# One fused attention and FFN layer: another order of head and loads, and a last FFN in token halves

## The chip, the cores and the metric

The kernel runs on one core of one Trainium2 chip. It is written for a scheduler that places instructions on five engines: TensorE (PE, matrix products), VectorE (DVE), ScalarE (ACT), GpSimd (POOL) and SyncE (SP, which here only issues transfers). The metric is the time on the device in microseconds (us), as a median of several runs. The profile is of one execution; its span is a little shorter than the time.

## The reference

What is computed, cut to what matters (`x` is 4 x 2048 tokens of 256 numbers, FFN weights are integers from -127 to 127):

```python
# attention within chunks of C = 32 tokens
Q = x @ W_q.T;  K = x @ W_k.T;  V = x @ W_v.T
decay = sigmoid(log_decay[0])
mask = where(diff >= 0, decay ** diff, 0)        # diff = position - position, 32 x 32
S = einsum('bncd,bnkd->bnck', Qc, Kc) * mask
O = einsum('bnck,bnkd->bncd', S, Vc)
gate = sigmoid(x @ W_g.T)
x = layernorm(x + ((gate * O) @ W_o.T + x))
# FFN with hidden size 768, weights scaled by 1/127
gate, up = x @ wg.T, x @ wu.T
x = layernorm(x + (silu(gate) * up) @ wd.T)
```

## The kernel before

The 8192 tokens are worked on in 16 blocks of 512. `Q K^T` is computed as `x (W_q^T W_k) x^T`, so a product `m` of the two weights is made once (`pm`), and a block needs `py` (x times m), `pg` (gate), `pv` (values), `ps` (scores), `po` (scores times values), `pa` (output product), then the first norm and `pt` (transposes). The FFN uses a faster single-pass format for its products. To keep precision, each activation is split in a high and a low part (`hT_hi`, `hT_lo`; `u_hi`, `u_lo`), and each product is done for both. The weights are exact integers there, as long as none is above 4096; the kernel counts the partitions with a larger one (`n_wide`) and would recompute everything in a second way if there were any.

Pools and banks (`bufs` is how many tiles of one name exist at once):

```python
xin = tc.tile_pool(name="xin", bufs=3)
work = tc.tile_pool(name="work", bufs=2)          # yT, sg, v, sT, goT, r, h, s, u, o ...
acts = tc.tile_pool(name="acts", bufs=H // P + 2) # u_hi, u_lo: 8 each
psum = tc.tile_pool(name="psum", bufs=8, space=PSUM)   # all products share 8 banks of 128 x 512
```

Loads at the start, in this order:

```python
wq = load_w(nc.sync, w_q, "wq")
wk = load_w(nc.scalar, w_k, "wk")
xs = {0: load_x(0)}                # xT, then x, both on nc.sync
wg = load_w(nc.scalar, w_gT, "wg")
wv = load_w(nc.scalar, w_vT, "wv")
nc.gpsimd.dma_start(decay, log_decay[0:1, 0:1].to_broadcast([P, 1]))
wo = load_w(nc.scalar, w_oT, "wo")
xs[1] = load_x(1)
ffn_int = [load_w(nc.sync, w, name) for ...]     # three of 768 KB
```

Then `pm` and its copy `m_sb`, the mask (some forty small DVE operations), and the loop:

```python
def integers(w_int, name):
    t = const.tile(list(w_int.shape), F32R, ...)
    nc.vector.tensor_copy(t, w_int)
    return t

def look_for_wide():
    for i, w_int in enumerate(ffn_int):
        nc.vector.tensor_reduce(top[:, i : i + 1], w_int..., ALU.max, apply_absolute_value=True)
    nc.vector.tensor_scalar(wide, top, EXACT, None, ALU.is_gt)
    nc.tensor.matmul(pw[:1, :3], lhsT=ones, rhs=wide, start=True, stop=True)
    nc.vector.tensor_reduce(count, pw[:1, :3], ..., ALU.add)
    nc.vector.tensor_copy(n_wide, count)

for b in range(-1, NB):            # attention of block n = b + 1 between parts of the FFN of b
    n = b + 1
    ffn, attn = b >= 0, n < NB
    ...
    if attn:
        yT, sg, v = attn_project(n)          # py, pg, pv
        sT = attn_scores(n, yT)              # ps
    if b == -1:
        fg, fu, fd = (integers(w, name) for ...)
        n_wide = look_for_wide()
    if ffn:  ffn_up(b, hT, uT, half[0])      # chunks 0 to 2 of the hidden size
    if attn: goT = attn_values(n, sT, v, sg) # po
    if ffn:  ffn_up(b, hT, uT, half[1])      # chunks 3 to 5
    if attn: h_next = attn_out(n, goT)       # pa, first norm
    if ffn:  r = ffn_down(b, uT, h)          # fdn
    if attn: h, hT = h_next, transpose_h(n, h_next)   # pt
    if ffn:  finish(b, r)                    # second norm, store of 512 KB
```

One chunk of the FFN, and the norm:

```python
# ffn_up, per chunk of 128 hidden units: fg and fu, 4 products of 512 columns each, then
nc.scalar.activation(s, pg, AF.Sigmoid, scale=SCALE)
nc.vector.tensor_tensor(s, pg, s, ALU.mult)
nc.vector.tensor_tensor(u, pu, s, ALU.mult)
nc.scalar.copy(hi, u)
nc.gpsimd.tensor_tensor(lo, u, hi.bitcast(F32), ALU.subtract)

# layer_norm, for the 4 groups of 128 tokens of a block
nc.vector.bn_stats(st, r[:, g, :]); nc.vector.bn_aggr(mv[:, g, :], st)     # per group
nc.scalar.activation(rstd, mv[:, :, 1], AF.Sqrt, bias=eps)                 # once
nc.vector.reciprocal(rstd, rstd)                                           # once
nc.vector.tensor_scalar(dst[:, g, :], r[:, g, :], mv..., rstd..., ALU.subtract, ALU.mult)  # per group
```

Of the kernel before, what the change touches and what calls it, by code (L numbers as in the profile page):

```python
# [34 lines left out]
P = 128  # L35
# [3 lines left out]
SCALE = 1.0 / 127.0  # L39
EXACT = 4096.0  # L40
EPS = 1e-5


@with_exitstack
def kernel(
# [32 lines left out]
        return psum.tile([P, TB], F32, tag="ps", name=name)  # L78


    def load_x(b, start=None):
        tokens = slice(b * TB, (b + 1) * TB) if start is None else bass.ds(start, TB)
        xt = xin.tile([P, KD, TB], F32, tag="xT", name=f"xT_{b}")
        nc.sync.dma_start(xt, xT[:, tokens].rearrange("(k p) t -> p k t", p=P))
        xn = xin.tile([P, NG, D], F32, tag="x", name=f"x_{b}")
        nc.sync.dma_start(xn, x[tokens, :].rearrange("(g p) d -> p g d", p=P))
        return xt, xn

    def load_w(eng, w, name):
        k, n = w.shape[0] // P, w.shape[1]  # L90
# [1 line left out]
        eng.dma_start(t, w.rearrange("(k p) n -> p k n", p=P))  # L92
        return t

    wq = load_w(nc.sync, w_q, "wq")
    wk = load_w(nc.scalar, w_k, "wk")
    xs = {0: load_x(0)}
    wg = load_w(nc.scalar, w_gT, "wg")
    wv = load_w(nc.scalar, w_vT, "wv")
    decay = const.tile([P, 1], F32, tag="decay", name="decay")  # L100
    nc.gpsimd.dma_start(decay, log_decay[0:1, 0:1].to_broadcast([P, 1]))
    wo = load_w(nc.scalar, w_oT, "wo")
    if NB > 1:
        xs[1] = load_x(1)
    ffn_int = [
        load_w(nc.sync, w, name)
        for w, name in ((ffn_gT, "fg_int"), (ffn_uT, "fu_int"), (ffn_dT, "fd_int"))
    ]

    ident = const.tile([P, P], F32, tag="ident", name="ident")  # L110
    make_identity(nc, ident)
# [2 lines left out]


    m_sb = const.tile([P, KD, D], F32, tag="m", name="m_sb")
    pm = bank("pm")
    for ec in range(KD):
        for dc in range(KD):
            nc.tensor.matmul(  # L120
                pm[:, ec * D : (ec + 1) * D],
                lhsT=wq[:, dc, ec * P : (ec + 1) * P],
                rhs=wk[:, dc, :],
                start=(dc == 0),
                stop=(dc == KD - 1),
            )
    nc.vector.tensor_copy(m_sb.rearrange("p k n -> p (k n)"), pm)  # L127

# [34 lines left out]

    def integers(w_int, name):
        t = const.tile(list(w_int.shape), F32R, tag=name, name=name)
        nc.vector.tensor_copy(t, w_int)
        return t

    def look_for_wide():

        top = const.tile([P, len(ffn_int)], F32, tag="top", name="top")
        for i, w_int in enumerate(ffn_int):
            nc.vector.tensor_reduce(  # L175
                top[:, i : i + 1],
                w_int.rearrange("p k n -> p (k n)"),
                mybir.AxisListType.X,
                ALU.max,
                apply_absolute_value=True,  # L180
            )
        wide = const.tile([P, len(ffn_int)], F32, tag="wide", name="wide")
        nc.vector.tensor_scalar(wide, top, EXACT, None, ALU.is_gt)
        ones = const.tile([P, 1], F32, tag="ones", name="ones")
        nc.vector.memset(ones, 1.0)
        pw = bank("pw")
        nc.tensor.matmul(pw[:1, : len(ffn_int)], lhsT=ones, rhs=wide, start=True, stop=True)
        count = const.tile([1, 1], F32, tag="count", name="count")
        nc.vector.tensor_reduce(
            count, pw[:1, : len(ffn_int)], mybir.AxisListType.X, ALU.add  # L190
        )
        n_wide = const.tile([1, 1], I32, tag="n_wide", name="n_wide")
        nc.vector.tensor_copy(n_wide, count)
        return n_wide

    def layer_norm(dst, r, name):

        mv = small.tile([P, NG, 2], F32, tag="mv", name=f"mv_{name}")
        for g in range(NG):
            st = small.tile([P, 6], F32, tag="st", name=f"st_{name}_{g}")  # L200
            nc.vector.bn_stats(st, r[:, g, :])
            nc.vector.bn_aggr(mv[:, g, :], st)
        rstd = small.tile([P, NG], F32, tag="rstd", name=f"rstd_{name}")
        nc.scalar.activation(rstd, mv[:, :, 1], AF.Sqrt, bias=eps)
        nc.vector.reciprocal(rstd, rstd)
        for g in range(NG):
            nc.vector.tensor_scalar(
                dst[:, g, :],
                r[:, g, :],
                mv[:, g, 0:1],  # L210
                rstd[:, g : g + 1],
                ALU.subtract,
                ALU.mult,
            )


    def attn_project(b):
        xt, _ = xs[b]
        yT = work.tile([P, KD, TB], F32, tag="yT", name=f"yT_{b}")
        sg = work.tile([P, KD, TB], F32, tag="sg", name=f"sg_{b}")  # L220
        v = work.tile([P, NG, D], F32, tag="v", name=f"v_{b}")
        for fc in range(KD):
            py = bank(f"py_{b}_{fc}")
            for ec in range(KD):
# [5 lines left out]
                    stop=(ec == KD - 1),  # L230
                )
            nc.vector.tensor_copy(yT[:, fc, :], py)
        for dc in range(KD):
            pg = bank(f"pg_{b}_{dc}")
            for ec in range(KD):
                nc.tensor.matmul(  # L236
                    pg,
                    lhsT=wg[:, ec, dc * P : (dc + 1) * P],
                    rhs=xt[:, ec, :],
                    start=(ec == 0),  # L240
                    stop=(ec == KD - 1),
                )
            nc.scalar.activation(sg[:, dc, :], pg, AF.Sigmoid)
        per = TB // D
        for h in range(NG // per):
            pv = bank(f"pv_{b}_{h}")
# [10 lines left out]
            nc.scalar.copy(  # L257
                v[:, h * per : (h + 1) * per, :].rearrange("p g d -> p (g d)"), pv
            )
        return yT, sg, v  # L260

    def attn_scores(b, yT):
        xt, _ = xs[b]
        ps = bank(f"ps_{b}")
        for g in range(NG):
            cols = slice(g * P, (g + 1) * P)
# [50 lines left out]
        return t[:, gs, :].rearrange("p g d -> p (g d)")  # L317

    def attn_out(b, goT):
        _, xn = xs.pop(b)  # L320
        r = work.tile([P, NG, D], F32, tag="r1", name=f"r1_{b}")

        def residual(gs, pb):
# [23 lines left out]
        return hi, lo  # L347


    def ffn_up(b, hT, uT, chunks):  # L350
        for hc in chunks:
            pg = bank(f"fg_{b}_{hc}")
            pu = bank(f"fu_{b}_{hc}")
            for pb, w in ((pg, fg), (pu, fu)):
                terms = [(dc, part) for dc in range(KD) for part in hT]
                for i, (dc, part) in enumerate(terms):
                    nc.tensor.matmul(  # L357
                        pb,
                        lhsT=w[:, dc, hc * P : (hc + 1) * P],
                        rhs=part[:, dc, :],  # L360
                        start=(i == 0),
                        stop=(i == len(terms) - 1),
                    )
            s = work.tile([P, TB], F32, tag="s", name=f"s_{b}_{hc}")
            nc.scalar.activation(s, pg, AF.Sigmoid, scale=SCALE)  # L365
            nc.vector.tensor_tensor(s, pg, s, ALU.mult)  # L366
            u = work.tile([P, TB], F32, tag="u", name=f"u_{b}_{hc}")
            nc.vector.tensor_tensor(u, pu, s, ALU.mult)  # L368
            hi = acts.tile([P, TB], F32R, tag="u_hi", name=f"u_hi_{b}_{hc}")
            lo = acts.tile([P, TB], F32R, tag="u_lo", name=f"u_lo_{b}_{hc}")  # L370
            nc.scalar.copy(hi, u)  # L371
            nc.gpsimd.tensor_tensor(lo, u, hi.bitcast(F32), ALU.subtract)  # L372
            uT[0].append(hi)
# [12 lines left out]
        return r  # L386

    def finish(b, r, start=None):
        tokens = slice(b * TB, (b + 1) * TB) if start is None else bass.ds(start, TB)
        o = work.tile([P, NG, D], F32, tag="o", name=f"o_{b}")  # L390
        layer_norm(o, r, f"f{b}")
        nc.sync.dma_start(
            out[tokens, :].rearrange("(g p) d -> p g d", p=P), o
        )


    half = list(range(KH // 2)), list(range(KH // 2, KH))
    h = hT = None
    for b in range(-1, NB):
        n = b + 1  # L400
        ffn, attn = b >= 0, n < NB
        if n + 1 < NB and n + 1 not in xs:
            xs[n + 1] = load_x(n + 1)
        if ffn:
            uT = [], []
        if attn:
            yT, sg, v = attn_project(n)
            sT = attn_scores(n, yT)
        if b == -1:
            fg, fu, fd = (  # L410
                integers(w, name) for w, name in zip(ffn_int, ("fg", "fu", "fd"))
            )
            n_wide = look_for_wide()
        if ffn:
            ffn_up(b, hT, uT, half[0])
        if attn:
            goT = attn_values(n, sT, v, sg)
        if ffn:
            ffn_up(b, hT, uT, half[1])
        if attn:  # L420
            h_next = attn_out(n, goT)
        if ffn:
            r = ffn_down(b, uT, h)
        if attn:
            h, hT = h_next, transpose_h(n, h_next)
        if ffn:
            finish(b, r)


    def wide_block(start, weights):  # L430

        wide_g, wide_u, wide_d = weights
        xs["w"] = load_x("w", start)
        yT, sg, v = attn_project("w")
        goT = attn_values("w", attn_scores("w", yT), v, sg)
        h = attn_out("w", goT)
        hT = work.tile([P, KD, TB], F32, tag="hT_hi", name="hT_w")
        for dc in range(KD):
# [86 lines left out]
```

## Time and profile before

| what | before |
|---|---|
| time, median of 3 runs | 599.48 us (598.05 to 599.63) |
| span of the profiled execution | 596.3 us |
| busy share of PE, DVE, ACT, POOL | 96%, 62%, 37%, 21% |
| mean granted clock of PE | 0.988 |
| transfers in the span | 29.36 MB, 49 GB/s on average |

The profile gives, for each engine, when it was busy and what released it after each wait. "PEld" is the load of stationary weights into TensorE, beside the products. A product of 32-bit numbers appears as two or more matmul records, and matmuls overlap, so that the pace from start to start is what counts and not the length of one record. A wait line names the engine and the tile that waited, whom it waited for, and the total, the number and the longest of the waits. The chain that ended last is followed back from the last instruction; in the order of time, each of its rows has a start, a length and what was done.

### The profile page before, as it was taken

How to read it: one execution, taken by the hardware profiler on the slowest of the kernel's cores; microseconds unless marked ns; L12 is line 12 of the kernel's file. 1: busy time of each engine (PE TensorE's matmuls, PEld its weight loads, DVE VectorE, ACT ScalarE, POOL GpSimd, SP SyncE). 2: the span in 40 equal slices, each digit the busy share in tenths (PEclk: the TensorE clock that was granted, in tenths of full speed). 3: DMA queues.
4: the chain of work that ended last, by engine and by line, in shares of the span. 5: the costliest groups of instructions: out<-in, count | busy, mean ns of one | idle time of the engine just before them, and what ended most of it. 6: DMA issues, size and time to landing. Idle time of an engine off the chain costs nothing.

```text
span 596.3 us, 7549 instructions
## 1 busy us (share of the span) xinstructions
PE 572.0 (96%) x2954; PEld 459.5 (77%) x2954; DVE 368.0 (62%) x843; ACT 220.6 (37%) x357; POOL 125.3 (21%) x107
## 2 busy tenths in 40 slices
PE   5589999999999999999999999999999999999994
PEld 3457878788787878878787896878878787887883
DVE  3853756748475674747568474765847477583784
ACT  0213335333343433334343333533333352334472
POOL 1000404022040412205031130502213040220422
PEclk9889999999999999999999999999999999999998
DMA  8611111211201111120211211021121101001011
GB/s 276 217 36 35 36 36 36 72 35 36 71 24 48 36 49 59 35 71 2 71 36 35 71 37 51 21 71 36 37 70 36 35 1 37 1 1 35 1 36 38
DMA packets 24006, 29.36 MB, mean 49 GB/s; under 512 B 928, under 2 KB 19360, under 8 KB 23968
## 3 DMA queue, kind: packets, MB, share of 16 engines
q1 hardware_dynamic: 22848, 27.79, 14.5%
q10 hardware_dynamic: 1088, 1.05, 0.5%
q8 instruction: 25, 0.41, 0.3%
q14 instruction: 13, 0.11, 0.1%
q0 software_dynamic: 32, 0.00, 0.0%
HBM read 20.45 MB, written 8.39 MB: 48 GB/s over the span
## 4 chain that ended last, share of the span: by engine, by line
PE 91%; DVE 4%; DMA 3%; ACT 1%; issue 0%; POOL 0%; POOLq 0%; SPq 0%; DVEq 0%
PE fdn L304 15%; PE fg L357 14%; PE fu L357 14%; PE pa L304 9%; PE py L225 9%; PE pv L250 9%; PE pg L236 9%; PE po L285 5%; PE ps L268 4%; PE pt L340 2%; DMA fg_int<-in_ffn_gT_dram 2%; DVE top L175 1%; DMA wk<-in_w_k_dram 1%; DVE u L368 0%; DVE mask L163 0%; DVE s L366 0%
## 5 line engine op out<-in xcount | busy, mean ns | idle before, releaser
L372 POOL TENSOR_TENSOR u_lo<-u,u_hi 128x512 fp32r<-128x512 f32 x96 | 123.4, 1285 | 458.7 <-ACT u_hi L371 458.2
L365 ACT ACTIVATE s<-fg 128x512 f32<-128x512 f32 x96 | 57.5, 599 | 106.4 <-PE fg L357 106.4
L366 DVE TENSOR_TENSOR s<-fg,s 128x512 f32<-128x512 f32 x96 | 66.4, 692 | 48.6 <-ACT s L365 48.6
L304 PE MATMUL fdn<-fd,u_hi 128*128 128x256 f32 x384 | 95.3, 292 | 0.0
L304 PE MATMUL fdn<-fd,u_lo 128*128 128x256 f32 x384 | 92.7, 280 | 1.2 <-POOL u_lo L372 1.2
L357 PE MATMUL fg<-hT_hi,fg 128*128 128x512 f32 x192 | 78.7, 410 | 0.2 <-ACT hT_hi L343 0.2
L357 PE MATMUL fu<-hT_hi,fu 128*128 128x512 f32 x192 | 76.3, 397 | 0.0
L357 PE MATMUL fg<-hT_lo,fg 128*128 128x512 f32 x192 | 76.1, 396 | 0.0
L357 PE MATMUL fu<-hT_lo,fu 128*128 128x512 f32 x192 | 76.0, 396 | 0.0
L276 DVE TENSOR_TENSOR sT<-ps,mask 128x512 f32<-128x512 f32 x16 | 11.1, 691 | 105.2 <-PE ps L268 105.2
L368 DVE TENSOR_TENSOR u<-fu,s 128x512 f32<-128x512 f32 x96 | 66.4, 692 | 13.1 <-DVE s L366 0.5
L304 PEld LDWEIGHTS fdn<-fd,u_lo 128*128 128x128 f32 x384 | 72.4, 189 | 2.0 <-POOL u_lo L372 1.6
L304 PEld LDWEIGHTS fdn<-fd,u_hi 128*128 128x128 f32 x384 | 71.8, 188 | 0.4
L371 ACT CAST u_hi<-u 128x512 fp32r<-128x512 f32 x96 | 59.0, 614 | 34.7 <-DVE u L368 34.7
L225 PE MATMUL py<-xT,m_sb 128*128 128x512 f32 x128 | 58.5, 600 | 1.0 <-DVE m_sb L127 1.0
L250 PEld LDWEIGHTS pv<-wv,xT 128*128 128x128 f32 x256 | 48.7, 190 | 13.4 <-issue 7.6
L304 PE MATMUL pa<-wo,goT 128*128 128x256 f32 x256 | 58.2, 380 | 0.0
L250 PE MATMUL pv<-wv,xT 128*128 128x256 f32 x256 | 57.9, 379 | 0.0
L236 PE MATMUL pg<-xT,wg 128*128 128x512 f32 x128 | 57.5, 593 | 0.0
L304 PEld LDWEIGHTS pa<-wo,goT 128*128 128x128 f32 x256 | 48.7, 191 | 7.3 <-DVE goT L292 0.4
L236 PEld LDWEIGHTS pg<-xT,wg 128*128 128x128 f32 x128 | 24.4, 190 | 30.6 <-issue 30.6
L357 PEld LDWEIGHTS fu<-hT_hi,fu 128*128 128x128 f32 x192 | 36.1, 188 | 8.8
(68 smaller groups left out, 657.9 us busy)
## 6 DMA issues: line engine op xcount, KB each, us to landing
xT<-in_xT_dram SPq DMA_DIRECT2D x16, 512.0 KB, 3.7
x<-in_x_dram SPq DMA_DIRECT2D x16, 512.0 KB, 3.6
out_dram<-o SPq DMA_DIRECT2D x16, 512.0 KB, 2.9
fg_int<-in_ffn_gT_dram SPq DMA_DIRECT2D x1, 768.0 KB, 10.9
fu_int<-in_ffn_uT_dram SPq DMA_DIRECT2D x1, 768.0 KB, 9.6
fd_int<-in_ffn_dT_dram SPq DMA_DIRECT2D x1, 768.0 KB, 11.4
wk<-in_w_k_dram ACTq DMA_DIRECT2D x1, 256.0 KB, 4.2
wq<-in_w_q_dram SPq DMA_DIRECT2D x1, 256.0 KB, 3.9
```

The costliest lines, as they stand in the source:

```text
L225: nc.tensor.matmul(py, lhsT=m_sb[:, ec, fc * P : (fc + 1) * P], rhs=xt[:, ec, :], start=(ec == 0), stop=(ec == KD - 1),)
L236: nc.tensor.matmul(pg, lhsT=wg[:, ec, dc * P : (dc + 1) * P], rhs=xt[:, ec, :], start=(ec == 0), stop=(ec == KD - 1),)
L250: nc.tensor.matmul(pv[:, j * D : (j + 1) * D], lhsT=xt[:, ec, g * P : (g + 1) * P], rhs=wv[:, ec, :], start=(ec == 0), stop=(ec == KD - 1),)
L268: nc.tensor.matmul(ps[:, cols], lhsT=xt[:, fc, cols], rhs=yT[:, fc, cols], start=(fc == 0), stop=(fc == KD - 1),)
L285: nc.tensor.matmul(po[:, cols], lhsT=v[:, g, dc * P : (dc + 1) * P], rhs=sT[:, cols], start=True, stop=True,)
L304: nc.tensor.matmul(pb[:, j * D : (j + 1) * D], lhsT=part[k][:, g * P : (g + 1) * P], rhs=w[:, k, :], start=(i == 0), stop=(i == len(terms) ...
L357: nc.tensor.matmul(pb, lhsT=w[:, dc, hc * P : (hc + 1) * P], rhs=part[:, dc, :], start=(i == 0), stop=(i == len(terms) - 1),)
L365: nc.scalar.activation(s, pg, AF.Sigmoid, scale=SCALE)
L366: nc.vector.tensor_tensor(s, pg, s, ALU.mult)
L368: nc.vector.tensor_tensor(u, pu, s, ALU.mult)
L371: nc.scalar.copy(hi, u)
L372: nc.gpsimd.tensor_tensor(lo, u, hi.bitcast(F32), ALU.subtract)
```

## The change

It leaves the work per block as it is and rearranges both ends of the kernel:

- **Loads in order of use.** The transposed `x` and the plain `x` become separate loads. `wg` and block 0's `xT` come first, then `wq`, `wk`, `wv`, block 1's `xT`, `wo`, and the rest. `decay` goes by the ACT queue instead of GpSimd's.
- **Products of zeros.** Two products on a tile of zeros go ahead of everything on TensorE, to keep it busy while the first loads are under way.
- **Order of the head.** Block 0's gate comes first, then the product of weights. Block 1's gate, `py`, `pv` and `ps` are put between the parts of block 0's attention, to give TensorE work where it waited for other engines.
- **Casts and check.** The casts of the FFN weights move from DVE to ACT, and the check for wide integers moves from the head into the turn b = 1, behind `finish`. Both are marked to keep their place in the program's order.
- **Last FFN.** It is done in two halves of 256 tokens, and residual, norm and store are done per 128 tokens, with stores issued by SP and ACT in turn.

The diff, cut to its core:

```diff
+WARM = 2
+    wg = load_w(nc.scalar, w_gT, "wg")
+    xTs[0] = load_xT(0)
+    nc.scalar.dma_start(decay, log_decay[0:1, 0:1].to_broadcast([P, 1]))
     wq = load_w(nc.sync, w_q, "wq")
     wk = load_w(nc.scalar, w_k, "wk")
-    xs = {0: load_x(0)}
-    wg = load_w(nc.scalar, w_gT, "wg")
     wv = load_w(nc.scalar, w_vT, "wv")
-    nc.gpsimd.dma_start(decay, log_decay[0:1, 0:1].to_broadcast([P, 1]))
+    xTs[1] = load_xT(1)
     wo = load_w(nc.scalar, w_oT, "wo")
-    xs[1] = load_x(1)
+    xns[0] = load_xn(0)
     ffn_int = [ ... ]
+    xns[1] = load_xn(1)
+    idle = const.tile([P, TB], F32, tag="idle", name="idle")
+    nc.vector.memset(idle, 0.0)
+    pi = bank("pi")
+    for _ in range(WARM):
+        nc.tensor.matmul(pi, lhsT=idle[:, :P], rhs=idle, start=True, stop=True)
 ...
     def integers(w_int, name):
-        nc.vector.tensor_copy(t, w_int)
+        tc.keep_in_program_order(nc.scalar.copy(t, w_int))
     def look_for_wide():
-            nc.vector.tensor_reduce(
+            reduced = nc.vector.tensor_reduce(
 ...
+            tc.keep_in_program_order(reduced)
 ...
+    def last_ffn(b, hT, h):
+        per = NG // 2
+        uTs = []
+        for half in range(2):
+            uT = [], []
+            ffn_up(b, hT, uT, range(KH), slice(half * per * P, (half + 1) * per * P))
+            uTs.append(uT)
+        for g in range(NG):
+            uT, t = uTs[g // per], g % per
+            pb = bank(f"fdn_{b}_{g}")[:, :D]
+            # 12 products of 256 columns: 6 chunks, high and low part
+            nc.vector.scalar_tensor_tensor(r[:, g, :], pb, SCALE**3, h[:, g, :], ALU.mult, ALU.add)
+            layer_norm(o, r, f"f{b}_{g}", [g])
+            eng = nc.sync if g % 2 else nc.scalar
+            eng.dma_start(out[b * TB + g * P : b * TB + (g + 1) * P, :], o[:, g, :])
 ...
-    for b in range(-1, NB):
+    sg = attn_gate(0)
+    make_m()
+    yT = attn_y(0)
+    v = attn_v(0)
+    sT = attn_scores(0, yT)
+    fg, fu = integers(ffn_int[0], "fg"), integers(ffn_int[1], "fu")
+    sg_next = attn_gate(1)
+    fd = integers(ffn_int[2], "fd")
+    goT = attn_values(0, sT, v, sg)
+    yT_next = attn_y(1)
+    h = attn_out(0, goT)
+    v_next = attn_v(1)
+    ahead[1] = sg_next, v_next, attn_scores(1, yT_next)
+    hT = transpose_h(0, h)
+    for b in range(NB - 1):
+        n = b + 1
+        ...                          # loads of block n + 1
+        if n in ahead: sg, v, sT = ahead.pop(n)
+        else: ...                    # attn_y, attn_gate, attn_v, attn_scores of n
+        ffn_up(b, hT, uT, half[0])
+        goT = attn_values(n, sT, v, sg)
+        ffn_up(b, hT, uT, half[1])
+        h_next = attn_out(n, goT)
+        r = ffn_down(b, uT, h)
+        h, hT = h_next, transpose_h(n, h_next)
+        finish(b, r)
+        if b == 1:
+            n_wide = look_for_wide()
+    last_ffn(NB - 1, hT, h)
```

## The prediction

> **What bounds the kernel now.** I read four views of the profile of before: the page's busy time, the chain that ended last in order of time, the waits by releaser, and the timelines of head and tail.
>
> ```profile
> PE 572.0 (96%) x2954; PEld 459.5 (77%) x2954; DVE 368.0 (62%) x843; ACT 220.6 (37%) x357; POOL 125.3 (21%) x107
> ...
> 76.68 3.44 PE py L225 x8
> 80.11 3.43 PE pg L236 x8
> 83.55 3.45 PE pv L250 x16
> 87.00 1.78 PE ps L268 x16
> ...
> 111.88 0.43 PE py L225
> ```
>
> TensorE (PE) is busy 96% of 596.3 us. The chain (start, duration, what) shows why: block 2's first projection `py` starts at 76.68 and block 3's at 111.88, so one turn of the loop takes 35.20 us, and the chain through it is matmuls alone. Nothing in the change makes a matmul of the middle cheaper. What can be won lies before 76.68 and after the last turn; and each PE wait put into the middle is lost whole, because PE has no slack there to recover it.
>
> The 76.68 us of head hold the attention of two blocks and the FFN of one. At full clock: two attentions at 3.44+3.43+3.45+1.78+1.78+3.45+0.87 = 18.2 each, the product of the two weights `pm` at 8 x 0.215 = 1.7, the FFN at 12 x 0.94 + 5.75 = 17.0. Sum 55.1. So 21.6 us are idle or slow. These rows name them (waits: total, times, longest; then the chain):
>
> ```profile
> PE pw L187 <- DVE wide L183: 6.2, 1, 6.2
> PE pm L120 <- DMA wk<-in_w_k_dram: 5.0, 1, 5.0
> PE pt L340 <- DVE h L207: 3.0, 1, 3.0
> PE py L225 <- DVE m_sb L127: 1.0, 1, 1.0
> ...
> 28.25 3.71 PE po L285 x16
> 31.96 2.43 PE pa L304 x10
> 38.63 2.10 PE pt L340 x8
> 40.72 4.19 PE py L225 x8
> ```
>
> 15.2 us are plain waits, the longest behind DVE: `pw`, the small matmul that counts wide integers, stands in PE's order ahead of everything that follows and needs three reductions. The rest is clock: `po` after that wait took 3.71 instead of 1.78, `pt` 2.10 instead of 0.87, `py` 4.19 instead of 3.44, and `pm` at the start 3.45 instead of 1.7.
>
> In the tail, the last matmul is in at about 588.7, and DVE then normalizes 512 tokens in one go until 592.4. The store is issued there:
>
> ```profile
> 582.57 1.29 POOL u_lo L372
> 585.31 1.83 PE fdn L304 x13
> 592.43 0.37 SPq L392 DMA_DIRECT2D out_dram<-o  x1
> ```
>
> **What the Trainium skill says.** "TensorE: Matmul & The Clock Gate", Part 1, has the array at half clock when cold, at full clock after some 3.4 us of work, and back at half after some 3.4 us idle. The trace agrees: `pm` starts cold, and `po` ran at half rate after 6.2 us of wait. The same page, Part 2, says matmuls stay in program order and only weight loads are pulled ahead. The trace agrees: `pw` waited, and `po` behind it with it. "ScalarE: Activation LUTs", What ACT_TABLE_LOAD costs, gives 1283 ns for a table load (here 1.28 us) and 186 ns + 0.833 ns per element for an activation; for 512 elements that is 613 ns, and `u_hi` takes 614 here. With it a 128x1536 cast is an estimated 1.47 us and a 128x256 one 0.40 us.
>
> **The change, part by part.**
>
> *Start.* The gate needs `wg` (256 KB) and `xT` of block 0 (512 KB), where `pm` needed 512 KB. Before, 512 KB had landed at 4.95 and all of `wq`, `wk`, `xT`, `wg`, 1.3 MB, at 8.76. By interpolation 786 KB land at about 6.2, and `wq` and `wk` still by 8.8. The products of zeros: memset 0.48 us, then 4 passes at 0.85 cold (twice the 0.43 of a full one), from about 1.45 to 4.9. They run inside the wait and should leave PE at full clock.
>
> *Block 0 and 1.* From 6.2 at full clock: `pg` 3.4, `pm` 1.7 (end 11.4), a wait of 1.0 for `m_sb` as before, `py` 3.4, `pv` 3.5, `ps` 1.8 (21.1), then block 1's `pg` to 24.5 (it covers mask and `sT`), `po` to 26.3, block 1's `py` to 29.7 (covers `goT`), `pa` to 33.2, block 1's `pv` and `ps` to 38.4. Block 0's norm takes some 4 us after `pa` (before: 35.7 to 39.4), so `pt` does not wait: 38.4 to 39.3. The FFN starts 1.27 after `pt` starts (568.44 to 569.71 in the last turn before): 39.7. The casts of the FFN weights, 3 x 1.47 on ScalarE (ACT) and no more on DVE, lie beside this. The rest of the turn is 35.2 less block 1's 12.1 = 23.1, and 0.2 for its start. Block 2's `py` starts at about 63.0 against 76.68: **13.7 won**.
>
> *The check for wide integers moves to the turn b = 1.* The order of the built kernel shows where: DVE runs the three reductions after all of `finish(1)`, and PE has `pw` right after `transpose_h` of block 2, ahead of block 3's `py`. By the timeline of DVE in a turn before:
>
> ```profile
> 147.37 1.27 DVE L344 TENSOR_TENSOR hT_lo<-pt,hT_hi 128x512 fp32r<-128x512 f32 x2
> ...
> 150.30 1.38 DVE L207 TENSOR_SCALAR o<-r,mv_f,rstd_f 128x256 f32<-128x256 f32 x4
> ```
>
> In this turn PE finished `pt` at 147.08 and went on with `py`. In after's turn it has to wait: the norm's end at 151.7 comes 0.4 sooner because no `yT` copy stands between (151.3); three reductions at 1.66 to 1.78 make 5.1 (156.4); `wide` and the semaphore 0.3 (156.7). That is 9.6 us of PE idle, plus 0.2 for `pw` itself, and the half clock after it, which after 6.2 us of wait cost 1.9 on `po` and 0.3 on `pa`: 2.0. So **11.8 lost**. At block 3's `py` the change stands at 98.2 + 11.8 = 110.0 against 111.88: 1.9 won.
>
> *The twelve turns from there* are the same instructions: 0.
>
> *Tail.* The two halves keep the matmul time: 96 up products of 256 columns at 0.12 (the pace of `fdn`) are 11.5 against 11.3. But a bank now holds half as much work, so PE can run only 4 chunks of 0.94 ahead instead of 4 of 1.87. ACT still loads three tables around block 14's norm; before it was clear for the second sigmoid only at 575.42. On that scale PE has used its eight banks at about 574.6 and waits some 1.5 for the first to be freed. Then DVE, at two operations per chunk (0.43 each, half of 0.69 plus the fixed part), takes 0.9 per chunk and holds PE to that pace: up ends near 583.0 instead of 581.0. The second half also needs 6 more pairs of `u_hi` and `u_lo` from 8 slots each: from its third chunk on they wait until `fdn_1` has read the first half's (584.5). Four `u_lo` of an estimated 0.7 on GpSimd (half of 1.285 and a little), with two `u` slots, bring the last one to 588.3 and the last matmul to about 590, against 588.7. Then the last 128 tokens: residual 0.4, statistics 0.6, root, reciprocal and scale 1.2 with two stores issued by ACT in between (0.5 each): last store issued near 593.2 against 592.43. Its 128 KB land faster than 512 KB (2.9), I take 2.2. Sum **0.1 lost**.
>
> Total: -13.7 + 11.8 + 0.1 = **-1.8 us**; from 599.48, **597.7 us**.
>
> **Rivals.** (a) *The check is hidden in the turn, as intended.* DVE is busy only 62%, which speaks for it; against it speaks that `pw` stands in PE's strict order, and that the same wait cost 6.2 before with PE just as able to do other work. It would make 599.5 - 13.6 = 586. (b) *The head gains less*: `xT` and `wg` land at 7 or later because both queues share the engines, and the warm-up falls badly against the clock's window, so `pg` starts cold (1.7 more). That is 2 to 3 us: about 600. (c) *The tail pays out*: if slots and banks bind less than I think, the norm per 128 tokens saves 2 to 3 (the chain after the last matmul was 3.7 plus a store of 512 KB): 595. If GpSimd's half tiles cost 1.0 instead of 0.7, the tail loses 1.5 more: 599.
>
> **Range and chances.** The loss behind `pw` I hold to 1.5 either way, the head to 2.5, the tail to 2; together about 3.5, and the runs before differ by 1.6. The range is 592.5 to 602.0. 2% is 12 us: faster by that needs rival (a), 0.06; slower by that needs new waits of more than 13 us, 0.02; within, 0.92.
>
> **What would show it.** Right: `pw` waits 9 to 10 us for `wide` just before block 3's `py`, which then takes over 5 us instead of 3.4; block 2's `py` starts near 63; `pm` takes 1.7; turns of 35.2 after that; PE waits for banks near the fifth chunk of the last FFN, and for `u_lo` in `fdn_2`. Wrong: a `pw` wait under 3 us (then rival a), block 2's `py` after 67, or a last matmul more than 3 us earlier or later after the last `pt` than the 20.3 us of before.

## The result, and the profile after

The time after is 598.73 us (median of 4 runs, 597.56 to 599.17); before, measured beside it, it is 598.86. The ratio is 0.9995, with a 95% interval of 0.9972 to 1.0018: no difference. The predicted time was 597.7. The profiled spans are 597.0 after and 596.3 before.

Three views show where the gain went. First the waits of PE in the profile after (engine, tile, line, whom it waited for; then total, times and longest, in us):

```profile
PE pw L208 <- DVE wide L204: 9.4, 1, 9.4
PE pi L126 <- DVE idle L123: 1.5, 1, 1.5
PE fg L389 <- DVE s L398: 1.2, 1, 1.2
PE pm L140 <- DMA wk<-in_w_k_dram: 1.0, 1, 1.0
PE py L262 <- DVE m_sb L147: 0.8, 1, 0.8
PE pg L246 <- DMA wg<-in_w_gT_dram: 0.6, 1, 0.6
...
PE fdn L443 <- POOL u_lo L404: 0.4, 1, 0.4
```

The 5.0 us for `wk` and the 3.0 for `h` have gone from the head. `pi` are the products of zeros; their 1.5 and the 0.6 lie inside the wait for the first load. The wait at `pw` has not gone: it has moved to another turn and grown from 6.2 to 9.4.

The chain of after in order of time (start, length, what) tells when. Its row of block 2's `py` answers to the 76.68 of before:

```profile
1.80 8.75 DMA wk<-in_w_k_dram
10.60 2.01 PE pm L140 x8
...
64.14 3.44 PE py L262 x8
...
102.10 1.38 DVE o L230 x4
103.48 4.99 DVE top L195 x3
108.91 6.55 PE py L262 x8
115.46 3.43 PE pg L246 x8
```

At 64.14 the change is 12.5 us ahead. Then the chain leaves PE for DVE: the scaling of block 1's output, three reductions (`top`), the comparison, `pw`. Block 3's `py` starts 3.0 ahead of before (108.9 against 111.88) and takes 6.6 instead of 3.44. The product after it starts at 115.46, against 111.88 + 3.44 = 115.32 before. Nothing is left of the head's gain.

The windows of after (from and to in us, busy time of PE, PEld, DVE, ACT and POOL with the number of instructions, granted clock of PE, share and rate of transfers) show the second part of the loss:

```profile
101.00:104.00 3.00, 0.00 (x0) 0.00 (x0) 2.56 (x8) 1.58 (x2) 0.00 (x0) 1.00 0.00 0
104.00:107.00 3.00, 0.00 (x0) 0.00 (x0) 3.00 (x3) 0.00 (x0) 0.00 (x0) 0.59 0.52 175
107.00:108.70 1.70, 0.00 (x0) 0.00 (x0) 1.63 (x2) 0.00 (x0) 0.00 (x0) 0.50 0.00 0
...
113.00:114.00 1.00, 1.00 (x2) 0.34 (x1) 0.35 (x1) 0.00 (x0) 0.00 (x0) 0.50 0.00 0
114.00:115.00 1.00, 1.00 (x3) 0.47 (x2) 0.00 (x0) 0.00 (x0) 0.00 (x0) 0.62 0.00 0
115.00:116.00 1.00, 1.00 (x4) 0.44 (x3) 0.50 (x1) 0.00 (x0) 0.00 (x0) 1.00 0.00 0
```

PE's last product ahead of `pw` ends at 99.3. The clock is still full up to 104 and 0.59 on average from 104 to 107, so it fell near 104.5, an estimated 5 us into the wait, if it went from full to half in one step. It stays at half for almost 6 us after PE is back at work.

The tail: the longest of the chain's rows of after between the last `pt` and the second half's products.

```profile
572.19 1.28 ACT L227
574.03 1.80 DVE o L230 x4
583.18 2.05 PE fdn L443 x17
```

and GpSimd in the timeline of after (start, busy time, line and operation; in brackets the idle time before):

```profile
585.31 1.44 POOL L404 TENSOR_TENSOR u_lo<-u,u_hi 128x256 fp32r<-128x256 f32 x2 [1.87 <-ACT u_hi L403]
587.08 1.43 POOL L404 TENSOR_TENSOR u_lo<-u,u_hi 128x256 fp32r<-128x256 f32 x2 [0.33 <-ACT u_hi L403]
```

From the start of the last `pt` to the end it is 28.4 us (568.59 to 597.0); before it was 27.9 (568.44 to 596.3). From the products at 583.18 the chain passes to GpSimd's `u_lo` at 585.3, whose slots are the tiles that these products have read; PE in turn waits 0.4 for `u_lo` (last row of the waits above). The last `u_lo` is done at 588.5, and the last 128 tokens are stored from 593.2 on.

The sum in the two profiles: head -12.5, check +12.7 (12.5 and the 0.14 by which the product after block 3's `py` starts late), tail +0.55; together +0.7, the difference of the spans.

### The profile page after: what moved, and what is told of

The parts are those of the page before. It is cut to its first block, busy times and chain, and to the rows that moved or that the text cites. A ratio compares the mean times of both kernels' runs of the same rounds, so it can differ in the third digit from the quotient of the medians.

```text
span 597.0 us, 7711 instructions
## 1 busy us (share of the span) xinstructions
PE 574.8 (96%) x3006; PEld 460.4 (77%) x3006; DVE 368.3 (62%) x858; ACT 226.7 (38%) x375; POOL 125.5 (21%) x112
## 4 chain that ended last, share of the span: by engine, by line
PE 93%; DVE 3%; DMA 2%; ACT 1%; issue 0%; POOL 0%; ACTq 0%; POOLq 0%
PE fg L389 15%; PE fu L389 15%; PE fdn L335 14%; PE py L262 10%; PE pv L281 9%; PE pa L335 9%; PE pg L246 9%; PE ps L299 5%; PE po L316 5%; PE pt L371 2%; DMA wk<-in_w_k_dram 1%; DVE top L195 1%; DVE o L230 1%; PE fdn L443 0%; DVE st_f L223 0%; PE pm L140 0%
## 5 line engine op out<-in xcount | busy, mean ns | idle before, releaser
L404 POOL TENSOR_TENSOR u_lo<-u,u_hi 128x512 fp32r<-128x512 f32 (+1 forms) x102 | 124.2, 1219 | 462.3 <-ACT u_hi L403 462.0
L397 ACT ACTIVATE s<-fg 128x512 f32<-128x512 f32 (+1 forms) x102 | 58.4, 573 | 104.5 <-PE fg L389 103.3
L398 DVE TENSOR_TENSOR s<-fg,s 128x512 f32<-128x512 f32 (+1 forms) x102 | 67.1, 658 | 48.4 <-ACT s L397 48.4
L389 PE MATMUL fg<-hT_hi,fg 128*128 128x512 f32 (+1 forms) x204 | 80.2, 396 | 1.6 <-DVE s L398 1.2
L389 PE MATMUL fu<-hT_hi,fu 128*128 128x512 f32 (+1 forms) x204 | 77.8, 384 | 0.0
L389 PE MATMUL fg<-hT_lo,fg 128*128 128x512 f32 (+1 forms) x204 | 77.7, 383 | 0.0
L389 PE MATMUL fu<-hT_lo,fu 128*128 128x512 f32 (+1 forms) x204 | 77.4, 382 | 0.0
L400 DVE TENSOR_TENSOR u<-fu,s 128x512 f32<-128x512 f32 (+1 forms) x102 | 67.1, 660 | 13.1 <-POOL u_lo L404 0.6
L403 ACT CAST u_hi<-u 128x512 fp32r<-128x512 f32 (+1 forms) x102 | 60.0, 589 | 36.2 <-DVE u L400 34.7
L389 PEld LDWEIGHTS fg<-hT_hi,fg 128*128 128x128 f32 x204 | 38.6, 189 | 9.2 <-DVE s L398 1.4
```

The source lines that it names most:

```text
L389: nc.tensor.matmul(pb, lhsT=w[:, dc, hc * P : (hc + 1) * P], rhs=part[:, dc, cols], start=(i == 0), stop=(i == len(terms) - 1),)
```

## The experiments

Each kernel was timed beside the kernel before on the same chip; ratios are to before, with their 95% intervals. "After" is the changed kernel.

**1. The count one turn later.** The reductions and the comparison stay in the turn b = 1; only the small product that needs them comes a turn later.

```diff
         nc.vector.tensor_scalar(wide, top, EXACT, None, ALU.is_gt)
+        return wide
+    def count_wide(wide):
 ...
         if b == 1:
-            n_wide = look_for_wide()
+            wide = look_for_wide()
+        if b == 2:
+            n_wide = count_wide(wide)
```

> The changed kernel with the check taken in two: the three reductions and the comparison stay behind finish(1), the counting matmul and what follows come one turn later, behind finish(2), where its input is long ready. Own theory: the wait of 9.4 us for the comparison, and the half clock behind it (block 3's py took 6.6 instead of 3.4), are what ate the head's gain; both vanish. The reductions hold DVE for 5.1 us, so block 3's yT copies come near 110 on the profile's scale, about when the scores need them, at most 1 us lost: about 586 to 587 us. Rival: it is not the wait but the 5 us of DVE work in a full turn that costs, and PE then waits for yT and for banks instead: 592 to 599 us.

Measured: 587.48 us, ratio 0.9817 [0.9804, 0.9830]. All the work is still there; one tiny product has moved. PE's longest waits are now

```profile
PE pi L126 <- DVE idle L123: 1.5, 1, 1.5
PE fg L392 <- DVE s L401: 1.2, 1, 1.2
PE pg L249 <- DMA wg<-in_w_gT_dram: 0.8, 1, 0.8
```

and in the chain of this kernel the two `py` are one plain turn apart, 35.20:

```profile
64.76 3.44 PE py L265 x8
...
99.96 3.44 PE py L265 x8
```

The rival, that the reductions' 5 us of DVE work hold PE up, is out: DVE has room for them. What cost 12.7 us was not their work but the place of `pw` in PE's order, ahead of block 3's `py`.

**2. The old check in the kernel before.** Before, with nothing changed but this: the reductions go behind `finish(1)` and the count behind `finish(2)`.

```diff
         if b == -1:
             fg, fu, fd = (integers(w, name) for ...)
-            n_wide = look_for_wide()
 ...
             finish(b, r)
+        if b == 1:
+            wide = look_for_wide()
+        if b == 2:
+            n_wide = count_wide(wide)
```

> The kernel before with nothing changed but the check: its reductions behind finish(1), its counting matmul behind finish(2). This shows how much of the head's gain was in the check alone. Own theory: in the head the first po then waits for the masked scores, behind casts and mask copies on DVE, to about 24.6 instead of 28.2, and the clock loss behind the wait shrinks by 1 to 2 us: 5 us faster, 594 us. Rival: DVE's casts and mask hold PE as long as the reductions did: 598 us; or all of the head's 12.5 us was the check: 586 us.

Measured: 592.17 us, ratio 0.9902 [0.9885, 0.9919], better than expected. The waits of PE in this kernel:

```profile
PE pm L120 <- DMA wk<-in_w_k_dram: 4.5, 1, 4.5
PE pt L344 <- DVE h L211: 3.0, 1, 3.0
PE po L289 <- DVE sT L280: 1.5, 1, 1.5
```

A wait of 1.5 at `po` comes up from beneath the one of 6.2 at `pw`, but with it the clock is kept: `po` takes 2.02 in the timeline, against 3.78 before. Block 2's `py` starts at 69.86, 6.8 before the 76.68. So of the gain more than half lay in the check alone. Load order, zeros, order of the parts and casts, less what the new tail costs (run 4), made up the rest, from 592.17 to 587.48; what each of them is worth was not tried.

**3. Zeros in the long wait.** After, with ten products of zeros put on PE ahead of `pw`. The wait stays; only the clock is kept up.

```diff
         if b == 1:
+            pf = bank("pf")
+            for _ in range(10):
+                nc.tensor.matmul(pf, lhsT=idle[:, :P], rhs=idle, start=True, stop=True)
             n_wide = look_for_wide()
```

> The changed kernel with ten products of zeros, of 0.86 us each at full clock, ahead of the counting matmul in the turn b = 1: the wait for the comparison stays as long as it is, but TensorE is busy through 8.6 of its 9.4 us. Own theory: the clock is what makes block 3's py take 6.6 us instead of 3.4, so py returns to 3.4 and 3.1 us are won: 595.5 us. Rival: products of zeros do not keep the clock up, or py is slow for another reason (its loads, its banks): 598.6 us.

Measured: 596.47 us, ratio 0.9964 [0.9950, 0.9977]. The timeline of PE there:

```profile
99.89 8.75 PE L503 MATMUL pf<-idle 128*128 128x512 f32 x20
109.44 0.19 PE L208 MATMUL pw<-wide,ones 128*1 128x3 f32 x2 [0.80 <-DVE wide L204]
109.56 3.70 PE L262 MATMUL py<-xT,m_sb 128*128 128x512 f32 x8
```

`py` takes 3.70 where it took 6.62 in after. So zeros keep the clock up, and 2.9 of the loss are the clock's and not the wait's. In the spans 2.2 come back (597.0 to 594.8), since in this execution block 2's `py` began 0.7 later. In the time it is about 1.9 (0.9995 less 0.9964, of 599), with intervals that overlap slightly. The size is not fixed: in the profiles of six kernels with the same 9.4 us of wait (after and runs 4 to 8), `py` took 6.62, 6.21, 5.19, 5.20, 5.24 and 5.23.

**4. The tail as before.** After, with the last turn of before.

```diff
-    last_ffn(NB - 1, hT, h)
+    b = NB - 1
+    uT = [], []
+    ffn_up(b, hT, uT, half[0])
+    ffn_up(b, hT, uT, half[1])
+    finish(b, ffn_down(b, uT, h))
```

> The changed kernel with the last turn of the kernel before: the last FFN whole, norm and store of 512 tokens at once. Own theory: the halves cost what they save (from the last transposes to the end 28.25 us against 27.86 before), so this is the same or up to 0.5 us faster: 598.3 us. Rival: the tail in halves does save 2 to 3 us and the profile's 0.4 us is chance: 601 us.

Measured: 598.10 us, ratio 0.9994 [0.9984, 1.0004], the same as after. From the last `pt` to the end its profile has 28.05 (567.85 to 595.9), against 28.4 in after. In the six profiles with this tail in halves (after and runs 1, 3, 7, 8 and 9) it is 28.4 to 29.2, in the three with the whole last turn (before and runs 2 and 4) 27.7 to 28.05. The token halves bring nothing; by the profiles they cost 0.4 to 1.5, which the times do not show.

**5. One wide tile for both halves.** After, with `u_hi` and `u_lo` of the last FFN as 512-wide tiles whose halves are written in turn: six tiles of each name instead of twelve for eight slots, so that nothing waits for a slot.

```diff
+        whole = [[acts.tile([P, TB], F32R, tag=t, ...) for hc in range(KH)] for t in ("u_hi", "u_lo")]
 ...
-            hi = acts.tile([P, n], F32R, tag="u_hi", name=f"u_hi_{b}_{hc}")
-            lo = acts.tile([P, n], F32R, tag="u_lo", name=f"u_lo_{b}_{hc}")
+            hi, lo = whole[0][hc][:, cols], whole[1][hc][:, cols]
```

> The changed kernel with the last FFN's two halves written into the two sides of the same 512-wide u_hi and u_lo tiles, so that the second half needs no further slots; nothing else moves. Own theory: the second half's last chunks no longer wait until fdn_1 has read the first half's tiles; the last u_lo comes some 2 us earlier, and so does the end: 596.7 us. Rival: DVE's and GpSimd's own pace sets the last u_lo, and the slots only look guilty: 598.3 us.

Measured: 597.93 us, ratio 0.9988 [0.9981, 0.9995]. In its chain the last products run through without a wait:

```profile
581.63 4.36 PE fdn L450 x36
```

From the last `pt` to the end it is 27.05 (567.05 to 594.1), 1.4 less than in after: the slots were what the tail paid. In the time only some 0.4 of that shows (0.9995 less 0.9988), with overlapping intervals, and less than the spread that the head makes (runs 10 to 12).

**6. The first sigmoid behind the root.** After loads ScalarE's table for the sigmoid, then the root's, then the sigmoid's again, because the first sigmoid of the last FFN comes ahead of block 14's root. Here it keeps its place in the program's order, behind the root.

```diff
-            nc.scalar.activation(s, pg, AF.Sigmoid, scale=SCALE)
+            sigmoid = nc.scalar.activation(s, pg, AF.Sigmoid, scale=SCALE)
+            if n < TB and hc == 0 and cols.start == 0:
+                tc.keep_in_program_order(sigmoid)
```

> The changed kernel with the first sigmoid of the last FFN kept behind the square root of block 14's norm on ACT: two table loads less between the first and the second sigmoid. Own theory: the second chunk's sigmoid then comes near 574 instead of 575.4 on the profile's scale, PE's wait for a free bank at the fifth chunk (1.2 us) goes, and with it 1 us of the end: 597.6 us. Rival: the slots of u_hi and u_lo set the end and take the gain back: 598.5 us.

Measured: 598.24 us, ratio 0.9991 [0.9983, 1.0000], not told apart from after by time. PE's wait for banks falls from 1.2 to 0.2, and the wait for slots is still behind it (timeline of PE in this kernel; the number in brackets is the wait):

```profile
574.07 0.39 PE L389 MATMUL fg<-hT_hi,fg 128*128 128x256 f32 x1 [0.23 <-DVE s L400]
586.58 0.39 PE L445 MATMUL fdn<-fd,u_lo 128*128 128x256 f32 x1 [0.43 <-POOL u_lo L406]
```

In this profile the slots do not take the gain back: from the last `pt` to the end it is 27.5 (568.31 to 595.8), 0.9 less than in after, and the last `u_lo` comes 1.0 sooner after `pt`. That is the 1 us of the own theory, and it is less than in any of the six profiles named in run 4.

**7. No zeros.** After without the products of zeros and their tile.

```diff
-    for _ in range(WARM):
-        nc.tensor.matmul(pi, lhsT=idle[:, :P], rhs=idle, start=True, stop=True)
```

> The changed kernel without the two products of zeros and their tile. Own theory: block 0's gate starts cold at 5.9 and takes about 5.2 us instead of 3.6, to 11.1; but the product of the two weights waits for wk until 10.55 anyway, so 0.5 us are lost: 599.2 us. Rival: the zeros also save the clock further on, up to 3 us lost: 601 to 602 us.

Measured: 599.59 us, ratio 1.0019 [1.0010, 1.0028], near the expected 599.2; the interval still overlaps that of after. Block 0's gate starts at 5.92 and takes 6.03, against 3.70 in after. `pm` then no longer waits for `wk`, so that block 2's `py` is only 1.1 later (65.22 against 64.14).

**8. `decay` behind `wk`.** After puts the load of `decay`, one number for each partition, ahead of `wk` on ScalarE's queue. Here it comes behind it, and ScalarE copies `m_sb`.

```diff
-    nc.scalar.dma_start(decay, log_decay[0:1, 0:1].to_broadcast([P, 1]))
     wk = load_w(nc.scalar, w_k, "wk")
+    nc.scalar.dma_start(decay, log_decay[0:1, 0:1].to_broadcast([P, 1]))
 ...
-        nc.vector.tensor_copy(m_sb.rearrange("p k n -> p (k n)"), pm)
+        nc.scalar.copy(m_sb.rearrange("p k n -> p (k n)"), pm)
```

> The changed kernel with the load of decay (128 pieces of 4 bytes) issued behind wk instead of ahead of it, and the copy m_sb done by ACT, so that DVE's mask chain, which decay now starts later, cannot hold it up. Own theory: decay's small pieces stand in the ACT queue ahead of wk and make the dip in the rate between 5.5 and 7 us; without them wk lands near 9.3 instead of 10.55, and the product of the weights starts when the gate ends, at 9.6: 1 us won, 597.7 us. Rival: the dip is there in the kernel before too, with decay on GpSimd's queue, and comes from something else, so that wk still lands at 10.5: 598.5 us.

Measured: 598.18 us, ratio 0.9994 [0.9981, 1.0007]: no gain in the time. In its profile `wk`, issued at 1.26, takes 6.7 to land, at 7.96 instead of 10.55, and `pm` follows the gate with no wait:

```profile
wk<-in_w_k_dram ACTq DMA_DIRECT2D x1, 256.0 KB, 6.7
```

```profile
5.98 3.70 PE L246 MATMUL pg<-xT,wg 128*128 128x512 f32 x8 [0.88 <-DMA wg<-in_w_gT_dram]
9.51 1.89 PE L140 MATMUL pm<-wk,wq 128*128 128x256 f32 x8
```

Block 2's `py` is at 62.83, 1.3 earlier than in after. The order of the two loads is what counts for `wk`: in the seven profiles with `decay` ahead of it (after, runs 1 and 3 to 7) it lands 8.4 to 9.0 after its issue, in the five with `decay` behind it (runs 8 to 12) 6.5 to 7.1. (`wk` is also issued 0.5 sooner then; what that alone does was not tried.) A dip in the rate of transfers is there in before too, as the rival had it (41 GB/s from 6.5 to 7.0 us), and stays here, only later and shallower: 68 GB/s from 6.0 to 6.5 in after, some 190 from 7.0 to 8.5 in this run; but `wk` is no longer behind it.

The 14 times of this kernel show how an earlier `wk` and an unchanged median go together: six lie between 596.61 and 597.11, eight between 598.09 and 600.51, and the profile is one of the first kind. What splits them is open: the gate's clock may do it, but the half clock behind `pw` is not of fixed size either (run 3). Runs 9 to 12 have no wait at `pw`.

**9. Two together.** Runs 1 and 8 in one kernel.

> The changed kernel with the counting matmul one turn behind its comparison and `decay` behind `wk` in its queue (and `m_sb` copied by ACT); the tail as it was. If an earlier `wk` reaches the end of the kernel now that nothing waits at `pw`: 586.2, 1.3 under the split alone (587.5). If the head's 1.3 are lost again elsewhere, as the time of the earlier run of it suggested: 587.0 to 587.5.

Measured: 586.47 us, ratio 0.9805 [0.9786, 0.9823], 1.0 under run 1, with overlapping intervals. Two of its times are at 585.5, two at 587.7 and 588.0, so that the median decides between neither expectation.

**10. Four together.** Runs 1, 5, 6 and 8 in one kernel.

> The changed kernel with four things together: the counting matmul one turn behind its comparison (that alone: 587.5), `decay` behind `wk` in its queue and `m_sb` copied by ACT (block 2's `py` 1.3 earlier), whole 512-wide `u_hi` and `u_lo` tiles in the last FFN (tail 1.3 shorter), and the first sigmoid of the last FFN behind block 14's root. If the parts add as their profiles have it: 587.5 - 1.3 - 1.3 - 0.3 = 584.6. If they add as their times alone had it (0.5, 0.6 and 0.4): 586.0. If they share a wait (the one for tile slots and the one for ScalarE's tables both end at the last product): 586.5. In the profile: no wait at `pw`, block 2's `py` near 62.9, last `pt` to end near 26.9.

Measured: 583.99 us, ratio 0.9770 [0.9753, 0.9787]; three times from 583.62 to 583.99, two at 585.7. That is 2.3% faster than before and the lowest median of all versions, not told apart from runs 11 and 12. All five times are under 586.0, so the parts add about as their profiles had it (584.6). From the last `pt` to the end it is 26.7 (554.90 to 581.6). The longest of PE's waits that are left:

```profile
PE pi L126 <- DVE idle L123: 1.5, 1, 1.5
PE py L265 <- ACT m_sb L147: 0.9, 1, 0.9
PE pg L249 <- DMA wg<-in_w_gT_dram: 0.8, 1, 0.8
PE fg L392 <- ACT hT_hi L377: 0.5, 2, 0.2
```

**11. Three products of zeros** in the combined version instead of two.

```diff
-WARM = 2
+WARM = 3
```

The window of 3.4 us in what was expected is the one cited in the prediction.

> The combined version with three products of zeros ahead of the gate instead of two. The five times of the combined version fall into two groups, 583.6 to 584.0 and 585.7, and in the profiles block 0's gate takes either 3.7 or 5.4 to 6.0. If that is the clock's window (two products of zeros last 3.8, hardly longer than one window of 3.4, so that only in some executions a whole window is busy before the gate starts): three last 5.1 at half clock, the gate takes 3.7 nearly always, at the price of a start up to 0.7 later; median 583.5 to 584.5, with at most one time near 585.7. If the groups come from the loads: two groups as before, the median anywhere from 583.5 to 586.

**12. No products of zeros** in the combined version (the edit of run 7).

> The combined version without products of zeros. If the clock's window makes the two groups: every time lies in the upper one or above it, 585.7 to 586.5, since the gate starts cold always and takes 6.0 instead of 3.7, and `pm` no longer waits for `wk` in that time; the profile has block 2's `py` near 65. If the groups come from the loads: two groups, 2 apart, whatever the zeros do.

Measured: with three 584.19 us, ratio 0.9755 [0.9740, 0.9769], five times from 583.34 to 584.36, none in the upper group. With none 584.84, ratio 0.9767 [0.9754, 0.9781], four times from 584.45 to 585.02 and one at 586.00. The gate of block 0 with three, then with none (timelines of PE):

```profile
1.47 5.25 PE L126 MATMUL pi<-idle 128*128 128x512 f32 x6 [1.47 <-DVE idle L123]
6.55 3.60 PE L249 MATMUL pg<-xT,wg 128*128 128x512 f32 x8
```

```profile
6.03 6.59 PE L244 MATMUL pg<-xT,wg 128*128 128x512 f32 x8 [6.03 <-DMA wg<-in_w_gT_dram]
```

The first theory, that the groups come from the clock, fits three products of zeros. It is not shown. No execution of run 10's upper group was profiled, and five times out of five in the lower group, where run 10 had three of five, can still be chance. Run 2, which has no zeros, falls into two groups about 2 us apart as well (591.03 to 591.39 and 592.95 to 593.46). For no zeros its forecast failed: it put every time at 585.7 or above, and four of the five lie about 1 below that, between the two groups. The one profiled, with the gate of 6.59, is the slowest.

The medians would put the two zeros at 0.85 us (584.84 less 583.99), but the ratios, 0.9767 and 0.9770, do not tell the two versions apart. Three are not told apart from two either (584.19 against 583.99); only the spread is less, 1.0 instead of 2.1.

## Why the prediction was right, point by point

The outcome was predicted: a large gain in the head, eaten by the check that was moved. The three terms came out at -12.5, +12.7 and +0.55, where -13.7, +11.8 and +0.1 were written. All three miss to the same side, by 2.5 together, and so 1.8 ahead became 0.7 behind in the spans; in the medians it is nothing either way. That the time of 598.73 lies so near the written 597.7 is in part luck: of the 1.8 us to be won nothing came, and the executions of before alone lie between 597.42 and 600.34.

- **Start of the head.** `wg` and `xT` landing at 6.2: measured 5.85. `pg` 3.4 at full clock: 3.70 in this profile. The step that failed is "`wq` and `wk` still by 8.8": `wk` landed at 10.55. The interpolation counted bytes and took the order of issue for the order of landing; run 8 shows that the small `decay` ahead of `wk` in the same queue held it up: with the two exchanged, `wk` was issued 0.5 and landed 2.6 us sooner (10.55 to 7.96). `pm`, expected to end at 11.4, ended at 12.6. With 0.2 less of wait for `m_sb` and 0.2 more in the stretch below, that is the head's 1.2.
- **Blocks 0 and 1.** From block 0's `py` (13.37) to block 2's (64.14) it took 50.8; written were 63.0 - 12.4 = 50.6. No PE wait above 0.2 is listed within that stretch: block 1's parts cover mask, `sT`, `goT` and the norm, and the casts on ScalarE took 1.46 to 1.48 against the estimate of 1.47.
- **Place of the check.** Right in kind and nearly in size: 9.4 of wait against 9.6. The reductions took 4.99 (written 5.1). The mis-sized term is the clock: "2.0", measured 3.1 (6.55 less 3.44 in the chains). It was carried over from a single observation, `po` and `pa` after the wait of before, and its parts, 1.9 and 0.3, make 2.2 and not 2.0. The place of block 3's `py` was also summed wrongly: the half clock falls into `py` itself, so that by the prediction's own numbers `py` starts at 108.0 and not at 110.0; it started at 108.9. The Trainium skill, "TensorE: Matmul & The Clock Gate", Part 1, calls the window of some 3.4 us free-running, not started by the kernel. Half clock of one to two windows costs half of that, an estimated 1.7 to 3.4. The traces agree: the losses by the chains, 1.7 in four profiles, 2.7 in one and 3.1 in after, all lie within it. A range should have been written there, not a number.
- **Middle.** 35.2 per turn from block 3's `pg` on, as written.
- **Tail.** Bank wait 1.2 against 1.5, up products done at 583.18 against 583.0, last `u_lo` at 588.5 against 588.3, last store issued at 593.2 as written. What is most off is the landing of the last 128 KB, 2.6 instead of 2.2. Run 5 confirms the cause of the cost: without slots to wait for, 1.4 less. Run 6 shows a second one, the order of the table loads: 0.9 less in its profile.
- **Rivals.** (a) was wrong for this change and right for the version in which only `pw` moves: 587.5, where 586 was written. (b) was the true direction of the head's miss, with another cause in the profiled run: the clock was up when `pg` started. In runs 1, 3 and 6, however, the profiles have `pg` at 5.43, 5.50 and 5.96, cold as (b) had it. (c) was out: 598.1 with the old tail.

So "same" does not mean that the change did little. Its intended gain is real, 11.0 us (run 1, 1.83% of 598.5), and is given back by one product with two records of 0.19 us in all, because what it waits for is the end of another engine's queue.

## What to carry to other kernels

A piece of side work moved off a crowded stretch is hidden only if its last consumer on the busy engine moves later still: put the producer in one turn and the consumer in the next. Read a strict in-order engine's order, not the idle share of the others, to see what a moved wait will hold up, and add the half clock behind it, here 1.7 to 3.1 us, to every wait that is long enough to lose the clock (here 3.0, 6.2 and 9.4). Load order has to be judged by landings: a tiny transfer in front of a large one in the same queue can cost more than its bytes, here some 2 us.

## What the runs showed of the hardware that was not expected

- **A few bytes delay a large load.** Behind `decay` (128 x 4 bytes) in its queue `wk` landed 8.8 us after its issue (8.4 to 9.0 in seven profiles), ahead of `decay` 6.7 (6.5 to 7.1 in five). The Trainium skill, "DMA: Bandwidth & Descriptors", Queues, rings and completion order, says that on each engine a queue's descriptors are consumed in ring order, which fits: `wk` was taken up behind `decay`. That this costs 2 us only the runs show. Why so small a load takes so long was not tried.
- **Two products of zeros bring the clock up only in some executions.** With two (3.4 to 3.8 us of products) block 0's gate took 3.7 in six profiles and 5.4 to 6.0 in three; with three (5.25 us) it took 3.6 in the one profile, and the five times lie within 1.0. That the slow gates ran at half clock is read from their pace alone: the granted clock of the profiles reads 1.00 in these microseconds, in after and in run 6 alike. The gate in the timelines of PE, of after and then of run 6:

```profile
5.85 3.70 PE L246 MATMUL pg<-xT,wg 128*128 128x512 f32 x8 [0.60 <-DMA wg<-in_w_gT_dram]
```

```profile
6.05 5.96 PE L246 MATMUL pg<-xT,wg 128*128 128x512 f32 x8 [0.80 <-DMA wg<-in_w_gT_dram]
```

- **Zeros count as work for the clock.** `py` after 8.75 us of them took 3.70, where it took 5.2 to 6.6 after as long an idle wait (run 3).
- **GpSimd and VectorE slow each other.** In the tail of after the four scalings of `o` took 1.80 with a `u_lo` beside them, 1.38 without (run 6). The `u_lo` took 0.88 instead of the 0.73 or 0.74 of others. The Trainium skill, "GPSIMD Engine Reference", 1. Specifications, lists the SBUF interfaces as shared with VectorE, with contention when VectorE's instruction is in a 2-port mode or has two inputs in SBUF. The slowing agrees; whether one of these conditions held here, no run shows. The lines are of after, DVE and POOL:

```profile
574.03 1.80 DVE L230 TENSOR_SCALAR o<-r,mv_f,rstd_f 128x256 f32<-128x256 f32 x4
574.16 0.88 POOL L404 TENSOR_TENSOR u_lo<-u,u_hi 128x256 fp32r<-128x256 f32 x1 [11.35 <-ACT u_hi L403]
```
